# Cross-attention: where the second group of scores stands between the weighted values and the projections of the next batch element

## The chip, the cores and the metric

The kernel runs on one core of a Trainium2 chip. The metric is the device time of one execution in microseconds (us); the median of several runs stands for a kernel. One further execution is taken by the hardware profiler; its trace gives the durations below.

The engines are called PE (matrix products; PEld is its loading of weights), DVE (vector), ACT (scalar, activation functions), POOL (general purpose) and SP (which issues most transfers). Each engine works through its own queue in order, and semaphores join the queues.

## What is computed

A decoder layer in float32: self-attention, cross-attention, and a mixture of experts, each behind a layer norm and each added to the residual. There are 8 batch elements of 112 tokens with 512 features. The change lies in the cross-attention, with 375 context tokens for each element and 32 heads of 16 features:

```python
q = x @ Wq.T
k_raw = context @ Wk.T
v_raw = context @ Wv.T
...
kv = jnp.concatenate([k_raw, v_raw], axis=-1)
kv = kv.reshape(b, m, NHEADS, HEAD_DIM, 2)
k = kv[..., 0].transpose(0, 2, 1, 3)
v = kv[..., 1].transpose(0, 2, 1, 3)
q = _rmsnorm(q)
k = _rmsnorm(k)
scores = jnp.einsum('bhnd,bhmd->bhnm', q, k) * scale
attn = jax.nn.softmax(scores, axis=-1)
out = jnp.einsum('bhnm,bhmd->bhnd', attn, v)
```

## The kernel before

The layer is one program in three stages: self-attention (to about 450 us of the profiled execution), cross-attention (to about 768 us), mixture of experts. In the cross-attention, queries of all tokens, and keys and values of the first element, are made ahead of the loop. The loop at lines 591 to 616 then works on element b and, between its pieces, makes keys and values of element b + 1.

A *pass* of the loop is an element b and a half cp of its 32 heads. A pass has three steps m, one for each third (125 tokens) of the context. Its parts, with the tiles by which the profile names them:

- `exp_scores(b, cp, m)`, line 503: the scores `xs` of 16 heads for one third of the context. A head has only 16 features, so the contraction is short: four strips of 32 rows of the PE array work side by side, each into its own PSUM buffer (line 511). ACT then takes the exponential of each strip (line 519) into a tile `e`. The strips come from the pool `sc`, which has four buffers, so one group of scores takes all of them until the exponentials have read them. The pool of `e` has five buffers (line 390).
- `weigh(b, cp, es)`, line 527: the weighted values `pv` of the pass *before*, from its three tiles `e`. Here the array is split by columns, 32 at a time (line 536). DVE copies the result out (line 551).
- `project_k(b + 1, m)` (line 423) in the first half and `project_v(b + 1, m)` (line 435) in the second: four float32 matmuls of 125 x 512 that use the full array. A key projection is copied out by ACT (`kraw`, line 405), squared by POOL (`sq`, line 407) and summed by DVE (`kss`, line 408); a value projection is copied out by DVE (line 442). The results go through the PSUM pool `mm`, of four buffers.
- `attend(b - 2)`, line 555, from the third element on, in the first half at m = 1: eight transposes `o_t` with the full array (line 561), then division by the softmax sums on DVE and an addition on POOL.
- after a second half, `spread_q(b + 1)` (line 472) and `normed_k(b + 1)` (line 484): the norms of the keys (a square root on ACT, line 411, a reciprocal and three multiplications on DVE) and the transposes `kT` (line 495), which ACT copies out (line 498).

Each matmul instruction of the program is float32 and appears in the profile as two records. A projection is thus "x8" there, a group of scores "x16", the weighted values "x96".

The order of the engines' queues is the program's, but for what a scheduler moves: it places the square root of line 411 and its table load earlier than the program does. On ACT they stand directly behind the third key projection's copy, and so ahead of the exponentials of the next pass, which need a table load of their own (the same instructions stand there for each element; the profile lists seven such loads for line 411).

The order on PE in one pass, when a pass is waiting to be weighted, is:

scores of third 0, weighted values of the pass before, projection 0, scores of third 1 (transposes of `attend`), projection 1, scores of third 2, projection 2.

Of the kernel before, what the change touches and what calls it, by code (L numbers as in the profile page):

```python
# [76 lines left out]
def decoder_layer(  # L77
# [39 lines left out]
    def psum(pool, name):  # L117
        return pool.tile([P, 512], F32, tag=pool.name, name=name)
# [6 lines left out]
    def load_ctx(b):  # L125
        t = ctxpool.tile([P, ND, M], F32, name=f"ctx{b}", tag="ctx")
        with tc.issue_after(first_weights):
            nc.sync.dma_start(out=t, in_=ctxT[b])
        return t
# [10 lines left out]
    def ln_rstd(mv, lo, hi):  # L140
        rs = lnpool.tile([P, TT], F32, tag="rs", name="rs")
        nc.scalar.activation(rs[:, lo:hi], mv[:, lo:hi, 1], AF.Sqrt, bias=eps_ln)
        nc.vector.reciprocal(rs[:, lo:hi], rs[:, lo:hi])
        return rs
# [6 lines left out]
    def ln_apply(mv, rs, t, xnT):  # L151
        xn = ln_normed(mv, rs, t)
        pt = psum(mm, "ln_t")
        for c in range(ND):
            nc.tensor.transpose(pt[:, c * P : (c + 1) * P], xn[:, c * P : (c + 1) * P], ident)
        nc.scalar.copy(xnT[:, :, t * P : (t + 1) * P], pt.rearrange("p (c s) -> p c s", c=ND))
# [227 lines left out]
    with ExitStack() as xa:  # L384
# [11 lines left out]
        ctxs = {0: load_ctx(0)}  # L396
# [6 lines left out]
        def head_squares(ps, n, dst, sums):  # L403

            nc.scalar.copy(dst, ps[:n, :])  # L405
            sq = krp.tile([P, 512], F32, tag="sq", name="sq", bufs=2)
            nc.gpsimd.tensor_tensor(sq[:n], dst, dst, ALU.mult)  # L407
            nc.vector.tensor_reduce(sums, sq[:n].rearrange("p (h d) -> p h d", h=XH), AX.X, ALU.add)
# [5 lines left out]
        def project_k(b, m):  # L414
            if m == 0:
                rawk[b] = (
                    krp.tile([MC, NM, 512], F32, tag="kraw", name="kraw"),
                    krp.tile([MC, NM, XH], F32, tag="kss", name="kss"),
                )
            k, ss = rawk[b]  # L420
            ps = psum(mm, "k")
            for c in range(ND):
                nc.tensor.matmul(  # L423
                    ps[:MC, :],
                    ctxs[b][:, c, m * MC : (m + 1) * MC],
                    wxk[:, c, :],
                    start=(c == 0),
                    stop=(c == ND - 1),
                )
            head_squares(ps, MC, k[:, m, :], ss[:, m, :])  # L430

        def project_v(b, m):
            ps = psum(mm, "xv")
            for c in range(ND):
                nc.tensor.matmul(  # L435
                    ps[:MC, :],
                    ctxs[b][:, c, m * MC : (m + 1) * MC],
                    wxv[:, c, :],
                    start=(c == 0),
                    stop=(c == ND - 1),  # L440
                )
            nc.vector.tensor_copy(
                values[b % 2][:, m, :, :XD], ps[:MC, :].rearrange("p (h d) -> p h d", h=XH)
            )
# [27 lines left out]
        def spread_q(b):  # L472

            queries[b] = qtp.tile([P, ND, 2, S], F32, tag="qT2", name="qT2")
            for e in range(2):
                nc.vector.tensor_scalar(
                    like_seq(queries[b][:, :, e, :], b),
                    seq(xn2, b),
                    cst[:, C_EO + e : C_EO + e + 1],
                    None,  # L480
                    ALU.mult,
                )
# [20 lines left out]
        def exp_scores(b, cp, m):  # L503


            e = ep.tile([MC, 2, 4, 2, S], F32, tag="e", name="e")
            strips = [psum(sc, f"xs{j}") for j in range(4)]
            for ci in range(2):
                for j in range(4):
                    rows = slice(32 * j, 32 * j + 32)  # L510
                    nc.tensor.matmul(  # L511
                        strips[j][:MC, ci * 2 * S : (ci + 1) * 2 * S],
                        keys[b][rows, 2 * cp + ci, m * MC : (m + 1) * MC],
                        queries[b][rows, 2 * cp + ci, :, :],
                        start=True,
                        stop=True,
                    )
            for j in range(4):
                nc.scalar.activation(  # L519
                    e[:, :, j, :, :].rearrange("p c e s -> p c (e s)"),  # L520
                    strips[j][:MC, : 4 * S].rearrange("p (c f) -> p c f", c=2),
                    AF.Exp,
                    scale=float(XD) ** -0.5,
                )
            return e

        def weigh(b, cp, es):


            ps = psum(mm, "pv")  # L530
            v = values[b % 2]
            for g in range(4):
                for m in range(NM):
                    for j in range(4):
                        h = 4 * g + j
                        nc.tensor.matmul(  # L536
                            ps[VW * j : VW * (j + 1), g * S : (g + 1) * S],
                            v[:, m, 16 * cp + h, :],
                            es[m][:, h // 8, (h % 8) // 2, h % 2, :],
                            start=(m == 0),  # L540
                            stop=(m == NM - 1),
                        )
            if cp == 0:
                if b == 0:
                    turned[0] = o0p.tile([P, 2, 4, S], F32, name="oT0")
                else:
                    turned[b] = otp.tile([P, 2, 4, P], F32, tag="oT", name="oT")
                    nc.gpsimd.tensor_copy(
                        turned[b][:, :, :, S:], turned[0][:, :, :, (b - 1) * SP : b * SP]
                    )  # L550
            nc.vector.tensor_copy(
                turned[b][:, cp, :, :S], ps[:, : 4 * S].rearrange("p (g s) -> p g s", g=4)
            )

        def attend(t):

            oT = turned.pop(t + 1)
            for cp in range(2):
                ps = psum(mm, "o_t")
                for g in range(4):  # L560
                    nc.tensor.transpose(ps[:, g * P : (g + 1) * P], oT[:, cp, g, :], ident)
                o = ps.rearrange("p (h d) -> p h d", h=16)
                r = op.tile([P, 16, 1], F32, tag="r", name="r")
                nc.vector.reciprocal(r, o[:, :, XD : XD + 1])
                w = op.tile([P, 16, XD], F32, tag="t", name="t")
                nc.vector.tensor_tensor(w, o[:, :, :XD], r.to_broadcast([P, 16, XD]), ALU.mult)
                half = xs[t][:, cp * 256 : (cp + 1) * 256]
                nc.gpsimd.tensor_tensor(half, half, w.rearrange("p h d -> p (h d)"), ALU.add)
            ln_stats(mv3, t)
# [20 lines left out]
        pending = None  # L590
        for b in range(B):
            for cp in range(2):
                es = []
                for m in range(NM):
                    es.append(exp_scores(b, cp, m))
                    if m == 0 and pending is not None:
                        weigh(*pending)

                    if m == 1 and cp == 0 and b >= 2:
                        attend(b - 2)  # L600
                    if b + 1 < B:
                        if cp == 0:
                            if m == 0:
                                ctxs[b + 1] = load_ctx(b + 1)
                            project_k(b + 1, m)
                        else:
                            project_v(b + 1, m)
                pending = (b, cp, es)
            if b + 1 < B:
                spread_q(b + 1)  # L610
                if b == 5:
                    rs3 = ln_rstd(mv3, 0, 4)
                normed_k(b + 1)
                if b == 5:
                    for t in range(4):
                        ln_apply(mv3, rs3, t, xn3)
# [448 lines left out]
```

## Time and profile before

| What | Value |
|---|---|
| median of 3 runs | 1041.7 us (1040.75 to 1043.2) |
| the profiled execution, its own time | 1046.2 us |
| span of the profiled execution (first to last instruction) | 1044.4 us |
| granted PE clock, mean over the span | 0.991 of full |
| share of the chain that ended last: PE / issue / DVE / DMA | 92% / 3% / 2% / 2% |
| `e` on ACT, line 519 | 192 instructions, 549 ns each, 88.9 us |
| `xs` on PE, line 511 | 768 records, 55.4 us |
| `xv` and `k` on PE, lines 435 and 423 | 192 records each, 88.4 and 87.6 us |
| the loop of the cross-attention | 503.8 to 767.6 us of the span |
| one element in the middle of it (638.05 to 672.60) | 34.55 us, PE busy 34.55, ACT 17.34, DVE 10.82, POOL 4.83 |
| the last element (744.20 to 767.60) | 23.40 us, PE busy 22.39, granted clock 0.78 |

An engine's busy time counts the stretches in which at least one of its instructions runs. PE's matmuls overlap, four at a time where the array is split, so a busy PE is not a PE at its peak. "Granted clock" is the share of the full PE clock that the chip allowed in a stretch. The *chain that ended last* follows the work back from the last instruction, at each step to what released it; the lengths of its pieces on one engine run from start to start, so they can be added. In the order of time, an entry in square brackets at the end of a line is the idle time before the instruction and what ended it.

### The profile page before, as it was taken

The numbers are of one execution on the slowest core, as the hardware profiler recorded it, in microseconds if no ns is written. First come the engines' busy times: TensorE is split into PE (matmuls) and PEld (weight loads), VectorE is DVE, ScalarE is ACT, GpSimd is POOL, SyncE is SP. The second block draws the span as 40 slices with busy tenths as digits, with TensorE's granted clock in tenths as the row PEclk, the third lists the DMA queues.
The fourth block names the chain that finished last, engine by engine and source line by source line (L and its number), as shares of the span: only waits on it lengthen the run. The fifth ranks groups of instructions, "written<-read, shape, count | busy, mean of one in ns | idle before, by whom it ended". The sixth has DMA issues, their size and how long they took to land.

```text
span 1044.4 us, 14683 instructions
## 1 busy us (share of the span) xinstructions
PE 1020.3 (98%) x5760; PEld 540.1 (52%) x5760; DVE 381.8 (37%) x744; ACT 277.4 (27%) x516; POOL 201.3 (19%) x223
## 2 busy tenths in 40 slices
PE   5999999999999999999999999999999989999988
PEld 3556555655565455645555555556665544444433
DVE  3345234522453244654223332242224133333223
ACT  2122011201120013123545554565532011111100
POOL 3241044103410221132100111011053200000041
PEclk9999999999999999999999999999989999999989
DMA  9421002101210120001000000001158247777664
GB/s 347 178 85 46 24 18 83 47 0 41 82 48 1 41 82 8 1 1 41 30 31 31 1 31 30 32 1 41 42 226 323 93 143 226 228 226 230 209 194 121
DMA packets 31092, 95.66 MB, mean 92 GB/s; under 512 B 3888, under 2 KB 5808, under 8 KB 27440
## 3 DMA queue, kind: packets, MB, share of 16 engines
q1 hardware_dynamic: 28272, 86.31, 24.7%
q0 software_dynamic: 2320, 7.63, 2.3%
q8 instruction: 46, 0.75, 0.3%
q10 hardware_dynamic: 432, 0.79, 0.2%
q14 instruction: 22, 0.18, 0.1%
HBM read 78.85 MB, written 14.94 MB: 90 GB/s over the span
## 4 chain that ended last, share of the span: by engine, by line
PE 92%; issue 3%; DVE 2%; DMA 2%; POOL 1%; ACT 0%; SPq 0%; DVEq 0%; POOLq 0%; ACTq 0%
PE qk L256 15%; PE o L343 9%; PE v L333 9%; PE xv L435 8%; PE k L423 8%; PE gu L645 6%; PE xs L511 5%; PE gate L876 4%; PE y L898 4%; PE pv L536 4%; PE up L876 4%; PE ys L924 4%; PE z L221 2%; PE s L186 2%; PE qk L311 1%
## 5 line engine op out<-in xcount | busy, mean ns | idle before, releaser
L519 ACT ACTIVATE e<-xs 125x448 f32<-125x448 f32 x192 | 88.9, 549 | 51.5 <-PE xs L511 51.3
L333 PE MATMUL v<-w,xn 128*128 128x512 f32 x224 | 100.4, 594 | 0.0
L343 PE MATMUL o<-wo,zT 128*128 128x512 f32 x224 | 99.9, 594 | 0.0
L435 PE MATMUL xv<-wx,ctx 128*125 128x512 f32 x192 | 88.4, 603 | 0.0
L423 PE MATMUL k<-wx,ctx 128*125 128x512 f32 x192 | 87.6, 601 | 0.0
L256 PE MATMUL qk<-xc,wc 128*128 128x448 f32 x180 | 70.1, 539 | 0.0
L645 PE MATMUL gu<-xn,sw 128*128 128x448 f32 x176 | 67.5, 540 | 0.0
L343 PEld LDWEIGHTS o<-wo,zT 128*128 128x128 f32 x224 | 41.0, 190 | 44.1 <-issue 44.0
L333 PEld LDWEIGHTS v<-w,xn 128*128 128x128 f32 x224 | 40.7, 190 | 42.1 <-issue 41.1
L407 POOL TENSOR_TENSOR sq<-kraw 125x512 f32<-125x512 f32 x24 | 25.2, 1050 | 184.9 <-ACT kraw L405 184.9
L511 PE MATMUL xs<-qT,kT 32*125 32x224 f32 x768 | 55.4, 380 | 1.0 <-ACT e L519 1.0
L876 PE MATMUL gate<-wex,xT 128*64 x144 | 56.0, 471 | 0.3 <-ACT xT L843 0.3
L423 PEld LDWEIGHTS k<-wx,ctx 128*125 128x125 f32 x192 | 34.3, 187 | 40.1 <-issue 40.1
L207 POOL TENSOR_TENSOR s<-s,sm 112x448 f32<-112x448 f32 x32 | 30.2, 943 | 128.9 <-DVE sm L206 101.3
L435 PEld LDWEIGHTS xv<-wx,ctx 128*125 128x125 f32 x192 | 34.1, 187 | 39.9 <-issue 39.9
L876 PE MATMUL up<-wex,xT 128*64 x144 | 54.4, 459 | 0.0
L511 PEld LDWEIGHTS xs<-qT,kT 32*125 32x125 f32 x768 | 36.6, 184 | 32.1 <-issue 27.6
L831 DVE COPY xn<-wex 128x704 f32 x60 | 31.2, 524 | 57.7 <-PE up L876 57.6
L909 POOL DMA_INDIRECT got<-routed,at x14 | 15.1, 1080 | 190.1 <-DMA routed<-y 186.1
L256 PEld LDWEIGHTS qk<-xc,wc 128*128 128x128 f32 x180 | 34.2, 190 | 33.5 <-issue 32.3
L256 PE MATMUL qk<-xn,w 128*128 128x448 f32 x120 | 50.2, 539 | 0.0
L898 PE MATMUL y<-wd,hT 128*64 128x512 f32 (+1 forms) x216 | 49.5, 592 | 0.6 <-ACT y L902 0.6
(181 smaller groups left out, 1475.2 us busy)
## 6 DMA issues: line engine op xcount, KB each, us to landing
wd<-in_wed_a SPq DMA_DIRECT2D x27, 512.0 KB, 3.7
wex<-in_wegu SPq DMA_DIRECT2D x8, 1408.0 KB, 17.0
wd<-in_wed_b SPq DMA_DIRECT2D x36, 192.0 KB, 4.5
w<-in_wqk SPq DMA_DIRECT2D x6, 1024.0 KB, 4.8
ctx<-in_ctxT SPq DMA_DIRECT2D x8, 750.0 KB, 4.2
slots<-zeros SPq DMA_DIRECT2D x1, 4608.0 KB
xt<-slots SPq DMA_DIRECT2D x18, 256.0 KB, 5.3
wd<-in_wed_a SPq DMA_DIRECT2D x18, 256.0 KB, 4.7
```

Of the source, the lines that this page charges most:

```text
L256: nc.tensor.matmul(ps[:, :HALF], wt[:, c * P : (c + 1) * P], x[:, c, :], start=(c == 0), stop=(c == 1))
L333: nc.tensor.matmul(ps, xn1[:, c, t * P : (t + 1) * P], wv[:, c, :], start=(c == 0), stop=(c == ND - 1))
L343: nc.tensor.matmul(ps, zT[:, h, t * P : (t + 1) * P], wog[:, h, :], start=(h == 0), stop=(h == GH - 1),)
L423: nc.tensor.matmul(ps[:MC, :], ctxs[b][:, c, m * MC : (m + 1) * MC], wxk[:, c, :], start=(c == 0), stop=(c == ND - 1),)
L435: nc.tensor.matmul(ps[:MC, :], ctxs[b][:, c, m * MC : (m + 1) * MC], wxv[:, c, :], start=(c == 0), stop=(c == ND - 1),)
L511: nc.tensor.matmul(strips[j][:MC, ci * 2 * S : (ci + 1) * 2 * S], keys[b][rows, 2 * cp + ci, m * MC : (m + 1) * MC], queries[b][rows, 2 * ...
L519: nc.scalar.activation(e[:, :, j, :, :].rearrange("p c e s -> p c (e s)"), strips[j][:MC, : 4 * S].rearrange("p (c f) -> p c f", c=2), AF.Exp,
L536: nc.tensor.matmul(ps[VW * j : VW * (j + 1), g * S : (g + 1) * S], v[:, m, 16 * cp + h, :], es[m][:, h // 8, (h % 8) // 2, h % 2, :], star ...
L645: nc.tensor.matmul(ps[:, :HALF], w[:, c, i % 2, k, :], xn3[:, c, cols], start=(c == 0), stop=(c == ND - 1))
L876: nc.tensor.matmul(gu[k][n, :FF], xT[:, c, n], w, start=(c == 0), stop=(c == ND - 1))
L898: nc.tensor.matmul(ps[n, :], hT[:fn, i, n], w[i][:fn], start=(i == 0), stop=(i == len(FCH) - 1))
L924: nc.tensor.matmul(p, hidden[n, i, t * P : (t + 1) * P], wsd_t[i // 3][n, i % 3, :], start=(i == 0), stop=(i == 5))
```

## The change

```diff
                     if m == 1 and cp == 0 and b >= 2:
                         attend(b - 2)
                     if b + 1 < B:
-                        if cp == 0:
-                            if m == 0:
-                                ctxs[b + 1] = load_ctx(b + 1)
-                            project_k(b + 1, m)
-                        else:
-                            project_v(b + 1, m)
+                        if cp == 0 and m == 0:
+                            ctxs[b + 1] = load_ctx(b + 1)
+
+
+                        for i in (range(m, m + 1) if pending is None else ((), (0,), (1, 2))[m]):
+                            (project_v if cp else project_k)(b + 1, i)
                 pending = (b, cp, es)
```

Where a pass before is waiting to be weighted (`pending`), step 0 makes no projection, step 1 makes projection 0, and step 2 makes projections 1 and 2. The order on PE in such a pass becomes:

scores of third 0, weighted values of the pass before, scores of third 1 (transposes of `attend`), projection 0, scores of third 2, projections 1 and 2.

The very first pass keeps its order, and the two passes of the last element have no projections. The load of the context stays where it was, at step 0 of the first half. The same instructions are issued. On ACT the copies of the key projections move with them: one behind the exponentials of the second third, two behind those of the last third, and the square root of line 411 with its table load stands behind these two as it stood behind the one. On DVE the sums `kss` and the copies of values move in the same way, and on POOL the squares. SP's queue is the same.

## The prediction

> Names used here: a pass is one (b, cp) of the loop at lines 591 and 592. Its three groups of scores (line 511) are S0, S1, S2, its weighted values (line 536) W, its three projections (line 423 where cp is 0, line 435 where cp is 1) P0, P1, P2. "First" and "second" passes have cp 0 and cp 1.
>
> **What bounds the kernel now.** I read the page's busy times first, then the chain of waits through one batch element, then ScalarE's order of time in the same stretch, then PE's order of time at the last element, and last the granted clock in single stretches.
>
> ```profile
> PE 1020.3 (98%) x5760; PEld 540.1 (52%) x5760; DVE 381.8 (37%) x744; ACT 277.4 (27%) x516; POOL 201.3 (19%) x223
> ```
>
> PE is never free, so whatever PE waits for newly is added to the end, and whatever PE does less of is taken off. The chain of waits (start, length, work; a piece runs to the start of the next) shows what a group costs and in which order they stand:
>
> ```profile
> 645.15 0.97 PE xs L511 x16
> 646.12 1.02 PE o_t L561 x8
> 647.14 3.43 PE k L423 x8
> 650.58 0.97 PE xs L511 x16
> 651.54 3.63 PE k L423 x8
> 655.17 0.97 PE xs L511 x16
> 656.14 2.44 PE pv L536 x96
> 658.57 3.63 PE xv L435 x8
> ```
>
> The reader should see two things. The same eight matmuls of a projection take 3.63 us behind scores and 3.43 us behind the transposes o_t, which use the same full array: changing the array's shape costs 0.20 us. And in the second pass, which begins at 655.17, S0 and W are over 3.40 us later; P0 comes next, and S1 only at 662.20.
>
> ScalarE in the same stretch (start, length, line, what):
>
> ```profile
> 639.16 1.85 ACT L519 ACTIVATE e<-xs 125x448 f32<-125x448 f32 x4 [0.33 <-PE xs L511]
> ...
> 655.21 0.59 ACT L405 COPY kraw<-k 125x512 f32<-125x512 f32 x1 [1.74 <-PE k L423]
> 655.81 1.28 ACT L411 ACT_TABLE_LOAD   x1
> 657.73 0.38 ACT L411 ACTIVATE kss<-kss,eps_rms 125x96 f32<-125x96 f32 x1 [0.64 <-DVE kss L408]
> 658.12 1.28 ACT L519 ACT_TABLE_LOAD   x1
> 659.42 1.85 ACT L519 ACTIVATE e<-xs 125x448 f32<-125x448 f32 x4
> ```
>
> This is what decides. In the first pass (S0 at 638.12) the four exponentials run at once and end at 641.01, just before W ends at 641.52. In the second pass they stand behind the copy of the last key projection, the square root of its norms and two table loads: they end at 659.42 + 1.85 = 661.27, that is 2.70 us after W's piece has ended (2.77 against PE's own start of the next group, 658.50, as the chain dates its pieces 0.07 later). The scores' PSUM pool has four buffers and each group fills all four, so S1 can't start until the exponentials of S0 free them, strip by strip. Today P0, 3.63 us long, covers that.
>
> PE's order of time at the last element, which has no projections, shows both outcomes:
>
> ```profile
> 747.59 1.04 PE L511 MATMUL xs<-qT,kT 32*125 32x224 f32 x16
> ...
> 761.33 2.93 PE L511 MATMUL xs<-qT,kT 32*125 32x224 f32 x16 [0.67 <-ACT e L519]
> 764.18 3.52 PE L536 MATMUL pv<-e,v 125*32 125x112 f32 x96
> ```
>
> At 747.59 S1 stands directly behind W, unhindered, at the usual length. At 761.33 scores stand directly behind scores: PE waits 0.67 us and then starts each strip 0.05 us after the exponential that frees it (the first ended at 761.27).
>
> **The change, part by part.** Sixteen passes; the very first keeps its order, the two of the last element have no projections, so 13 change: 6 first ones (b = 1 to 6) and 7 second ones (b = 0 to 6). Instructions are the same in kind and number.
>
> *Removed: one change of shape.* S0, W, P0, S1, P1, S2, P2 become S0, W, S1, P0, S2, P1+P2; the transposes of line 561 stay behind S1, next to a projection. The new step from W to S1 costs no more than the others (the group at 747.59 has its usual 1.04). 13 x 0.20 = 2.6 us less.
>
> *New: S1 directly behind W.* In the six first passes the fourth exponential is over 0.44 us before W is (641.01 against 641.45, PE's own start of the next group; at b = 6, where ScalarE has LayerNorm copies ahead, 0.76): no wait. In the seven second passes the fourth exponential ends 2.70 us (b = 0, 1) or 2.77 us (b = 2 to 6) after PE could start S1. That end is unmoved by the change: it hangs on the end of P2 of the pass before, through copy, square, sum, square root and loads, and in the changed kernel's order ScalarE still has copy, copy, load, square root, load, exponentials there. With 0.05 us for the release, less the 0.02 us by which the fourth strip starts after the first anyway, the wait is 2.73 or 2.80 us: 2 x 2.73 + 5 x 2.80 = 19.5 us. Behind the waiting matmuls stand P0, S2, P1 and P2 on the in-order PE; nothing gives this back, since PE has no idle time later in the element.
>
> *New: the clock.* Waiting may cost more than its length. The stretches below (length, busy times, granted clock, DMA):
>
> ```profile
> 759.49:762.91 3.42, 2.75 (x34) 1.83 (x30) 0.62 (x1) 1.85 (x4) 0.00 (x0) 1.00 0.00 0
> 762.91:766.32 3.41, 3.41 (x58) 2.81 (x58) 0.00 (x0) 2.68 (x5) 0.00 (x0) 0.50 0.00 0
> 844.83:848.24 3.41, 1.94 (x12) 0.70 (x8) 1.49 (x3) 0.46 (x1) 0.00 (x0) 1.00 0.83 252
> 848.24:851.65 3.41, 2.53 (x17) 1.46 (x18) 0.53 (x1) 0.59 (x1) 0.00 (x0) 1.00 0.27 58
> ```
>
> The clock changes on a grid of 3.41 us. In the first stretch PE was idle for 0.67 us and then ran one strip of four for 1.31 us (each busy 0.37 of 0.43 us, so 0.21 of the array: 1.03 us of array time lost): 1.70 us lost, and the next stretch got half the clock. In the third 3.41 - 1.94 = 1.47 us were lost and the clock stayed. The threshold lies between. The predicted wait loses 1.51 us idle (658.50 to 660.01, the first release), 1.03 in the trickle and 0.28 in the tail of the fourth strip: 2.8 us. Only a grid line that splits it so that neither side passes the threshold spares it. With the threshold at 1.70 that is a line 1.12 to 1.75 us into the wait, 0.63 of 3.41 us, so 82% trip; at 1.47 it is 0.12 us, 96%. I take the middle, 89% or 6.2 of 7. A trip's price from the same place: W took 3.52 for the usual 2.51 us (+1.0), and the scores before it reached W 1.55 us after their last release (762.63) where 0.95 is usual (+0.6): 1.6 us; bounds are 1.5 and the 1.71 of a whole stretch at half. 6.2 x 1.6 = 10.0 us, between 8.6 (5.7 x 1.5) and 11.5 (6.7 x 1.71).
>
> [...] The trace shows half clock after stretches that were idle for only 0.67 us, so I go by the row.
>
> *Moved at no cost.* P1 and P2 stand together, with the four-buffer pool of line 117 under them: the buffer that each takes belonged to work that ended over 2 us earlier, against copies of 0.6 to 0.7 us. The copies of keys on ScalarE come after S2's exponentials (1.85 us), inside P1's 3.43. The element's last projection still ends where the next S0 starts, so the norms, the transposes kT and the next keys are due as before. POOL's squares stand three in a row behind its additions, about 1.04 us each against 3.43 us a projection; SP's order, with the context load, is unchanged. A fifth buffer for exponentials exists for S1 (five are named at line 390). If one of these covers failed it would cost at most the 0.6 us of a copy in a pass.
>
> **Sum.** -2.6 + 19.5 + 10.0 = +26.9 us. The profiled execution took 1046.2 us (span 1044.4) and would become 1073.1; it lies 4.5 us over the median of the runs, 1041.7, which becomes 1068.6.
>
> **Rivals.**
> - *The wait alone, full clock* (16%): 1041.7 - 2.6 + 19.5 = 1058.6. For it: the 1.47 us stretch that didn't trip. Against it: two trips at the last element with 0.33 and 0.67 us of plain idleness.
> - *Each trip lasts two stretches* (11%): the first trip at the last element held from 752.67 to 759.49, 6.82 us. 6.2 x 3.3 = 20.5, so 1079. Against it: there scores still trickled in its first stretch, here a dense projection follows.
> - *No wait, only the saved shape* (3%): 1041.7 - 2.6 = 1039.1. It decides if S0's exponentials in the second passes end by 658.5 and not 661.3, so if the square root and its loads, 2.9 us of ScalarE's time with the sum they wait for, leave that place. For it: S1 at 747.59 and the six first passes. Against it: the order named above.
> - *No measurable change* (2%): the waits are eaten by slack that I don't see; PE's idle time in the whole span is 24 us, 1044.4 - 1020.3, and hardly any lies here.
>
> **How the numbers follow.** The forecast has 68%, with its own range 1065 to 1072 (the trips' bounds, and 1.5 us for the runs' spread of 1040.75 to 1043.2). The range must take in the second-likeliest case at 1058.6 and stops short of the two-stretch case: 1057 to 1074. A difference under 0.2% (2 us) can't be told from none. Faster 3%, within 2%, slower 95%.
>
> **What would show it.** In the chain: W followed by xs with an idle entry released by ACT e at every second pass, 1.5 us, groups of about 3.8 us with their wait in place of 0.97, none in first passes; P1+P2 as one piece of 16 matmuls and 7.06 us; granted clock 0.50 for 3.41 us after most of the seven. Busy PE times grow where the clock halves. I am wrong if the second passes show no such idle entry, or if the clock stays at 1.00 through them.

## The result, and the profile after

The changed kernel took 1072.99 us (median of 6 runs, 1069.59 to 1074.99), the kernel before 1041.22 (6 runs, 1039.59 to 1044.59): 1.0298 of it, 95% interval 1.0271 to 1.0324, so 31.8 us more. Foretold were +26.9 us, 1068.6, within 1057 to 1074; the measured time lies above the 1065 to 1072 that the forecast gave to its likeliest case. The profiled execution of the changed kernel has a span of 1071.0 us, that of the kernel before 1044.4. These two differ by only 26.6 us, because the profiled execution of before (1046.2 us) was slower than every one of its six timed runs; the closeness to 26.9 is chance. In two runs below a single execution took 2128 and 3033 us at full clock; the medians given leave these two out.

The names are those of the prediction: S0, S1, S2 are a pass's groups of scores, W its weighted values, P0 to P2 its projections. PE's order of time in the changed kernel shows one second pass (cp = 1, from 671.87) and the start of the next element; columns are start, length, engine, line, operation, and in brackets the idle time before it and who ended it:

```profile
671.87 1.04 PE L511 MATMUL xs<-qT,kT 32*125 32x224 f32 x16
672.84 2.51 PE L536 MATMUL pv<-e,v 125*32 125x112 f32 x96
676.72 2.55 PE L511 MATMUL xs<-qT,kT 32*125 32x224 f32 x16 [1.37 <-ACT e L519]
679.20 5.12 PE L435 MATMUL xv<-wx,ctx 128*125 128x512 f32 x8
684.25 1.04 PE L511 MATMUL xs<-qT,kT 32*125 32x224 f32 x16
685.22 7.13 PE L435 MATMUL xv<-wx,ctx 128*125 128x512 f32 x16
692.18 1.45 PE L495 MATMUL kT<-cst,kraw 125*128 125x125 f32 x12
693.56 1.04 PE L511 MATMUL xs<-qT,kT 32*125 32x224 f32 x16
694.53 2.51 PE L536 MATMUL pv<-e,v 125*32 125x112 f32 x96
696.97 1.04 PE L511 MATMUL xs<-qT,kT 32*125 32x224 f32 x16
```

S1 at 676.72 has the idle entry that was foretold (1.37 us, where 1.5 was expected), and takes 2.55 us for the usual 1.04: its four strips start one by one, 0.43 to 0.44 us apart (676.72, 677.15, 677.59, 678.03). P0 behind it takes 5.12 us for the usual 3.70. P1 and P2 are one piece of 16 records. The next first pass (693.56) has W and S1 back to back and no wait.

The chain of waits ran on PE alone through this loop before, up to the last element. Now it leaves PE once in each second pass as well, and names every step that the exponentials waited for:

```profile
666.79 5.16 PE k L423 x12
671.95 0.02 issue
671.98 0.59 ACT kraw L405
672.57 0.07 issue
672.64 1.05 POOL sq L407
673.69 0.02 issue
673.71 0.70 DVE kss L408
674.41 0.03 issue
674.43 0.02 ACT kss L411
674.46 0.37 issue
674.83 1.28 ACT L519
676.11 0.01 issue
676.12 0.55 ACT e L519
676.67 0.04 issue
676.72 2.55 PE xs L511 x16
679.27 5.05 PE xv L435 x8
```

From the end of P2, 671.95, it runs over the keys' copy, square, sum, square root (dated as issue, 674.46) and table load to the first exponential, then to S1. S0 and W, which PE works off meanwhile (672 to 675.3), are not in the chain: they have become the shorter way.

The profile records when the granted clock changed. In the changed kernel it went between 1.00 and 0.50 at 18 times, from 521.67 to 1033.67 us of the span, and any two of these lie a whole number of times 3.41 us apart; so do the 7 times in the kernel before, from 752.67 to 1042.80. These times, carried on every 3.41 us through a profile, are called its grid here; the word describes these records and no more.

The windows (length, then busy times of PE, PEld, DVE, ACT, POOL with their numbers of instructions, granted clock, DMA share, GB/s), first the second passes of b = 0, 1 and 2, then four stretches of the grid about the wait of b = 1:

```profile
515.23:536.91 21.68, 20.31 (x181) 11.61 (x180) 6.76 (x11) 9.83 (x18) 1.04 (x1) 0.92 0.02 3
552.94:576.32 23.38, 22.01 (x181) 12.20 (x180) 6.76 (x11) 9.82 (x18) 1.04 (x1) 0.85 0.03 4
593.18:614.87 21.69, 20.32 (x182) 11.48 (x181) 6.77 (x11) 9.83 (x18) 1.04 (x1) 0.92 0.02 3
...
555.81:559.22 3.41, 2.04 (x38) 1.35 (x30) 3.18 (x5) 3.20 (x6) 0.00 (x0) 1.00 0.00 0
559.22:562.63 3.41, 3.41 (x13) 1.79 (x13) 0.00 (x0) 1.85 (x4) 0.00 (x0) 0.50 0.01 2
562.63:566.05 3.42, 3.42 (x5) 1.32 (x4) 0.00 (x0) 0.00 (x0) 0.00 (x0) 0.50 0.00 0
566.05:569.46 3.41, 3.41 (x23) 1.63 (x22) 1.51 (x3) 1.34 (x4) 0.00 (x0) 1.00 0.00 0
```

A second pass took 17.51 us before (551.43 to 568.94 at b = 1). It takes 21.7 us where the clock was halved for one stretch and 23.4 where it was for two, as here from 559.22 to 566.05. Over the loop, from its first scores to the end of the last W, the profiles give 263.7 us before (503.92 to 767.63) and 294.45 after (501.44 to 795.89), +30.7 us. It comes together like this, all from PE's starts:

| Where | Change, us |
|---|---|
| six first passes, 0.19 to 0.20 each (at b = 1, 16.22 became 16.03) | -1.2 |
| seven second passes: +4.17, 5.87, 4.18, 5.77, 4.19, 5.69, 4.24 | +34.1 |
| the last element, 744.18 to 767.63 became 774.67 to 795.89 | -2.2 |

Of the +34.1, the waits are 7 x 2.75 = 19.3 (at b = 6, where the clock fell only after the wait, P0 starts 2.72 us late; at b = 2, 2.77), the saved changes of shape -1.4, and what is left, 16.2, is put down to the clock (the runs with useless work, below, check this): four passes with one slow stretch (1.6 us each), three with two (3.1 to 3.3).

### The profile page after: what moved, and what is told of

The parts are those of the page before. It is cut to its first block, busy times and chain, and to the rows that moved or that the text cites. A ratio compares the mean times of both kernels' runs of the same rounds, so it can differ in the third digit from the quotient of the medians.

```text
span 1071.0 us, 14683 instructions
## 1 busy us (share of the span) xinstructions
PE 1037.4 (97%) x5760; PEld 550.0 (51%) x5760; DVE 382.1 (36%) x744; ACT 277.4 (26%) x516; POOL 200.9 (19%) x223
## 4 chain that ended last, share of the span: by engine, by line
PE 86%; issue 5%; ACT 2%; DMA 2%; DVE 2%; POOL 2%; SPq 0%; DVEq 0%; POOLq 0%; ACTq 0%
PE qk L256 15%; PE o L343 9%; PE v L333 9%; PE xv L435 8%; PE k L423 6%; PE gu L645 6%; PE xs L511 5%; PE gate L876 4%; PE y L898 4%; PE up L876 4%; PE ys L924 3%; PE pv L536 2%; PE z L221 2%; PE s L186 2%; POOL sq L407 2%
## 5 line engine op out<-in xcount | busy, mean ns | idle before, releaser
L435 PE MATMUL xv<-wx,ctx 128*125 128x512 f32 x192 | 99.7, 674 | 0.0
L511 PE MATMUL xs<-qT,kT 32*125 32x224 f32 x768 | 66.4, 389 | 10.6 <-ACT e L519 10.6
L435 PEld LDWEIGHTS xv<-wx,ctx 128*125 128x125 f32 x192 | 39.7, 215 | 51.5 <-issue 51.5
L511 PEld LDWEIGHTS xs<-qT,kT 32*125 32x125 f32 x768 | 43.3, 186 | 37.8 <-issue 18.6
L442 DVE COPY v<-xv 125x512 f32<-125x512 f32 x24 | 16.6, 692 | 93.8 <-PE xv L435 93.8
## 6 DMA issues: line engine op xcount, KB each, us to landing
slots<-zeros SPq DMA_DIRECT2D x1, 4608.0 KB, 19.3
```

The lines of the kernel that those rows point to most:

```text
L435: nc.tensor.matmul(ps[:MC, :], ctxs[b][:, c, m * MC : (m + 1) * MC], wxv[:, c, :], start=(c == 0), stop=(c == ND - 1),)
L511: nc.tensor.matmul(strips[j][:MC, ci * 2 * S : (ci + 1) * 2 * S], keys[b][rows, 2 * cp + ci, m * MC : (m + 1) * MC], queries[b][rows, 2 * ...
```

## Experiments

Two theories were set against each other. *Wait and clock*: in second passes S1 waits for exponentials that stand on ScalarE behind the square root of the keys' norms, and the granted clock goes to 0.50 after the wait, as it did after the two waits of the last element before. *Neighbours*: what now stands side by side (scores behind weighted values, two projections in a row with their copies) costs something of its own in every changed pass. Each ratio is to runs of the kernel before on the same chip.

**First passes alone.**

```diff
-for i in (range(m, m + 1) if pending is None else ((), (0,), (1, 2))[m]):
+for i in (range(m, m + 1) if pending is None or cp == 1 else ((), (0,), (1, 2))[m]):
```

> The new order in the first passes alone (cp = 0, six of them); the second passes keep the order of before. If the loss is the wait for the exponentials behind the square root (with the halved clock after it), the first passes never wait and only six changes of shape at 0.20 us are saved: 1041.2 - 1.2 = 1040.0 us, no idle entry before a group of scores up to the last element, clock 1.00 there. If instead the new neighbours cost something of their own (scores directly behind the weighted values, or two projections in a row with their copies), six of thirteen passes pay it: 1041.2 + 6/13 x 31.8 = 1056 us.

Measured: 1040.33 us (12 runs), 0.9984 of the kernel before (0.9968 to 0.9999). In the element from 637 to 672 us PE has no idle entry, and the granted clock was 0.998 over the span, as one stretch of 3.41 us at 0.50 makes it. Six passes in the new order are a small gain, by about the six changes of shape (0.0016 x 1042 = 1.7 us, interval 0.1 to 3.3, for 1.2 expected). In first passes the neighbours cost nothing.

**Second passes alone.** The same edit with `cp == 0`.

> The new order in the second passes alone (cp = 1, seven of them). If the loss is the wait and the clock: seven waits of 2.8 us and seven trips as in the changed kernel, less seven changes of shape only: 1073.0 + 1.2 = 1074 us, give or take 3 us for where the clock's grid falls. If the neighbours cost: 1041.2 + 7/13 x 31.8 = 1058 us.

Measured: 1073.67 us (median of 3 runs), 1.0295 (1.0263 to 1.0326): the whole loss, in seven passes of thirteen. One of the seven waits went by at full clock; the windows are the two stretches of that profile's grid about it:

```profile
677.33:680.74 3.41, 1.97 (x65) 1.58 (x55) 2.93 (x5) 2.77 (x5) 0.00 (x0) 1.00 0.00 0
680.74:684.15 3.41, 3.41 (x19) 2.00 (x19) 0.82 (x2) 2.58 (x6) 0.00 (x0) 1.00 0.00 0
```

The grid line, 680.74, fell 2.03 us into the wait (W was over at 678.71): 1.51 idle and 0.52 x 0.79 = 0.41 of trickle, 1.92 us of array time lost ahead of it by the prediction's count, and the clock stayed at 1.00.

**The square root later.** The changed kernel, with ScalarE's square root of the keys' norms ordered behind the exponentials of the second pass's S0:

```diff
...
+    with tc.issue_after(last_exp[b - 1, 1, 0]):
+        nc.scalar.activation(flat_kss, flat_kss, AF.Sqrt, bias=eps_rms[:MC], scale=1.0 / XD)
...
```

> The changed kernel with one more order on ScalarE: the square root of the keys' norms, with its table load, stands behind the exponentials of the second pass's first group of scores and no longer ahead of them. All instructions stay. If that place is the cause, the exponentials end 2.97 us after the group's start, before the weighted values are over at 3.40 us: no wait, no halved clock in the seven passes, all thirteen changes of shape saved: 1041.2 - 2.6 = 1038.6 us. If the neighbours or the projections in a row cost, it stays at 1073 us. If only half of the wait goes (the loads then hold up the second group's exponentials against the third scores, margin by my sum 0.2 us), between 1040 and 1050 us.

Measured: 1038.44 us (12 runs), 0.9968 (0.9954 to 0.9983). No instruction was added or taken, nothing on PE was reordered against the changed kernel, and over 30 us are gone. The chain of waits in a second pass is PE's alone again:

```profile
653.20 0.97 PE xs L519 x16
654.17 2.44 PE pv L544 x96
656.60 0.97 PE xs L519 x16
657.57 3.63 PE xv L435 x8
661.20 0.97 PE xs L519 x16
662.16 7.06 PE xv L435 x16
```

S1 (656.60) follows W at once, in 0.97 us. ScalarE in that stretch has the exponentials at 654.24, and the loads and the square root behind them:

```profile
654.24 1.85 ACT L527 ACTIVATE e<-xs 125x448 f32<-125x448 f32 x4 [0.42 <-PE xs L519]
656.11 1.28 ACT L491 ACT_TABLE_LOAD   x1
657.41 0.38 ACT L491 ACTIVATE kss<-kss,eps_rms 125x96 f32<-125x96 f32 x1
657.80 1.28 ACT L527 ACT_TABLE_LOAD   x1
659.10 1.85 ACT L527 ACTIVATE e<-xs 125x448 f32<-125x448 f32 x4
```

**The control: the same on the kernel before.**

> The control: the kernel before with the square root moved in the same way. There the first projection of 3.63 us already covers the exponentials, so nothing waits for the square root: 1041.2 us, no change within 1 us. If moving the square root were a gain of its own, it would show here as in the run beside it: about 1038.6 us.

Measured: 1042.05 us (median of 11 runs), 0.9999 (0.9981 to 1.0017). The place of the square root is worth nothing by itself. What the last two runs together show is the change without its wait: a gain of about 3 us, for 2.6 worked out.

**Useless work in the wait.** The changed kernel, with matmuls between W and S1 of the second passes whose result nobody reads:

```diff
+if cp == 1 and b + 1 < B:
+    idle = psum(mm, "idle")
+    for _ in range(3):
+        nc.tensor.matmul(idle, ctxs[b][:, 0, :P], wxv[:, 0, :], start=True, stop=True)
```

> The changed kernel with useless work in the wait: in the seven second passes three more matmuls of 128 x 512 with the full array (six records of 0.43 us, and a change of shape of 0.20, so 2.77 us) between the weighted values and the second group of scores; their result is not read. If the wait of 2.8 us and the clock are the loss, this work takes the wait's place and keeps PE busy: no idle entry, no halved clock in the seven passes: 1041.2 - 2.6 + 7 x 2.8 = 1058 us, so more work and 15 us less time than the changed kernel. If the loss were work of PE's own (shape changes, neighbours), the 19 us of added work come on top: 1092 us.

> The same with two useless matmuls (1.72 us and one change of shape, 1.92). The wait that is left is 0.88 us and falls into the trickle of the strips; the second group still starts its fourth strip at the same time, so the sum is again 1058 us, and by the threshold of 1.47 to 1.70 us of lost array time no clock is halved (0.88 x 0.79 + 0.28 = 1.0 us lost). If a trip needs no such threshold, 10 us more.

> The same with one useless matmul (0.86 us and one change of shape, 1.06). The wait that is left loses 0.45 us idle, 1.03 in the trickle and 0.28 in the tail, 1.76 us: just over the threshold, and only if one grid stretch holds nearly all of it. Few trips, 0 to 3 of seven: 1058 to 1063 us. If the length of the plain idle time decided, and not the array time lost, 0.45 us would never trip; if any wait tripped, seven would: 1069 to 1074 us.

Measured, in this order: 1059.37 us, 1.0165 (1.0136 to 1.0194); 1056.89 us, 1.0151 (1.0117 to 1.0186); 1060.74 us, 1.0175 (1.0147 to 1.0203). All three take some 12 to 16 us less than the changed kernel, though each does more. PE's order with three and with one such matmul, and the clock with three and with one, from 500 to 762 us, which takes in all seven of these passes' waits:

```profile
665.77 2.51 PE L536 MATMUL pv<-e,v 125*32 125x112 f32 x96
668.20 2.84 PE L601 MATMUL idle<-wx,ctx 128*128 128x512 f32 x6
670.98 1.04 PE L511 MATMUL xs<-qT,kT 32*125 32x224 f32 x16
671.94 3.70 PE L435 MATMUL xv<-wx,ctx 128*125 128x512 f32 x8
```

```profile
665.71 2.51 PE L536 MATMUL pv<-e,v 125*32 125x112 f32 x96
668.15 1.12 PE L601 MATMUL idle<-wx,ctx 128*128 128x512 f32 x2
669.59 2.32 PE L511 MATMUL xs<-qT,kT 32*125 32x224 f32 x16 [0.32 <-ACT e L519]
671.85 3.70 PE L435 MATMUL xv<-wx,ctx 128*125 128x512 f32 x8
```

```profile
500.00:762.00 262.00, 262.00 (x2467) 144.40 (x2465) 75.68 (x136) 128.17 (x240) 30.89 (x38) 1.00 0.07 24
```

```profile
500.00:762.00 262.00, 259.76 (x2439) 144.92 (x2437) 75.65 (x136) 128.19 (x240) 30.89 (x38) 1.00 0.07 24
```

P0 starts as late as ever (three: 671.94 - 665.77 = 6.17 us after W's start; one: 6.14; the changed kernel's P0 679.20 - 672.84 = 6.36, part of it at half clock), but takes 3.70 us, and the clock is 1.00 through all seven waits. This separates the two terms: with the wait's length kept and the clock kept up, the loss is about 17 us; the rest of the 31.8, some 15, is the clock's. By passes it comes out the same: with one useless matmul a second pass, from its W to the next (six of the seven; the other holds LayerNorm work), takes 2.73 us more than in the run with the later square root (20.04 against 17.31), the wait alone; in the changed kernel it takes 21.7 or 23.3. With one useless matmul, idleness and trickle still lose 1.7 us a pass (estimated with the prediction's count), and the clock was halved after none of the seven waits.

**Useful work in the wait.** P0 of the second passes in halves, two of its four matmuls ahead of S1:

```diff
...
+if cp == 1 and b + 1 < B:
+    project_v(b + 1, 0, range(2))
...
+if cp and i == 0:
+    project_v(b + 1, 0, range(2, ND))
...
```

> The changed kernel with useful work in the wait: in the seven second passes the first two of projection 0's four matmuls stand between the weighted values and the second group of scores, the other two behind it. Seven groups of one shape again in these passes. 1.72 + 0.20 us of the wait are covered, 0.88 is left, no halved clock: 1041.2 - 1.2 + 7 x 0.88 = 1046 us. If the two projections in a row at the pass's end were a loss of their own, it would stay above 1055 us.

Measured: 1043.94 us (10 runs), 1.001 (0.999 to 1.003). S1 takes 1.85 us for 1.04 in the second passes (0.81 x 7 = 5.7 us, less 1.2 for the shapes), and in its profile the clock was full over the whole loop, the last element too (1.0 over the span), where the profile of before loses time to two trips. That explains in these two executions why it cost less than foretold (the loops take 264.5 and 263.7 us); the other runs were not profiled. P1 and P2 in a row do no harm here either.

**The lesson tried on the last element.** It has no projections, so its own S0 waits for the exponentials of S2. The last third of its value projection was kept back to stand between them, on top of the later square root:

```diff
...
+if cp and b + 1 == B - 1 and i == 2:
+    continue
...
+elif cp == 0 and m == 2:
+    project_v(b, m)
```

> The changed kernel with the square root later (as in the run before), and the same lesson used on the last element, which has no projections to cover its exponentials: the last third of its own value projection (due only in the second pass of that element) stands behind the third group of scores of its first pass, and no longer in the element before. If a wait for exponentials costs its length and a halved clock, the wait between these two groups of scores (0.33 us idle and the trickle, 1.6 us in all) and the first of the two trips there (about 1.6 us) go, and two changes of shape come in (0.4 us): 2.8 us under the run beside it, 1035.6 us. If the last element's slow clock is not the waits' doing, only 1.2 us.

> The kernel with the square root later once more, on the same chip as the run beside it: 0.9968 of the kernel before, about 1038.5 us.

Measured: 1037.13 us, 0.9941 (0.992 to 0.9962), beside 1036.10 us, 0.9936 (0.9913 to 0.9959), for the kernel without it: no gain in the time. In the profiles it is there at first: the last W of the loop ends at 759.72 instead of 762.39, 2.7 us earlier where 2.8 were foretold, with no halved clock in that element (granted clock 1.00 from 740 to 770 us, beside 0.94). But the experts' stage then runs two slow stretches more of 3.41 us than the kernel beside it (from 841.5 us on one, from 995.0 two for one; granted clock 0.97 beside 0.99 from 840 to 1000 us, 0.93 beside 0.98 from there on), and the spans are 1037.7 and 1037.4. Whether that is chance in these two executions or follows from the shifted start is open; the runs' medians show no gain.

The fastest kernel found is thus the change with the square root later: 0.9968 and 0.9936 of the kernel before on two chips, 1038.44 and 1036.10 us. The last kernel (0.9941) can't be told from it.

## Why the prediction was right, and what it mis-sized

*The change of shape, -2.6 us.* Right: 0.19 to 0.20 us less in each first pass, and the run with the later square root gains about that over its control.

*The wait, +19.5 us.* Right: 7 x 2.75 = 19.3. It was read from where the fourth exponential stood against the end of W in the trace of before, and from the order on ScalarE, which the change leaves alone. The first passes, where 0.44 us of margin were read, never waited.

*Only in second passes, and for the square root's sake.* Right, and shown: the loss stays with the second passes alone, leaves with the square root's place, and that place is worth nothing without the change.

*The clock, +10.0 us, between 8.6 and 11.5.* That the waits would be followed by half the clock was right (seven waits with 1.37 us of plain idle time each, granted clock 0.50 in the next stretch after all seven), and the size was not: 16.2 us. Two steps failed.

- "A trip's price from the same place ... 1.6 us; bounds are 1.5 and the 1.71 of a whole stretch at half" held for four of seven. Three trips lasted two stretches and cost 3.1 to 3.3 us. The prediction had this as a rival that holds for all trips or for none. What goes with the one or the other is where the grid's line fell in the wait. In the changed kernel, lines 2.41 to 2.87 us into the wait (three) went with two slow stretches, and lines 3.04 to 4.27 us into it (four) with one. In the three, P0 starts only 1.56 to 2.12 us into the first slow stretch, with the rest of S1 before it; in the four, at most 1.24 us into it.
- "82% trip; at 1.47 it is 0.12 us, 96%" took the grid's line as drawn anew for each wait, and 1.47 to 1.70 us of lost array time as what decides. The upper bound was mis-sized: 1.70 counted only the idleness and the trickle of its stretch, and in the run with second passes alone 1.92 us by the same count left the clock at 1.00. An estimate from the two traces of before and after counts every matmul record for as long as its columns take (0.43 us for 512 at full clock, as in a projection) and for its share of the array; it gives 2.19 us for the prediction's stretch. By this estimate, of 160 stretches of the grid at full clock from 500 to 800 us in the two profiles, the ten that were followed by a halved one had lost 2.19 to 2.71 us of their 3.41, and the other 150 at most 1.82. With 1.92 to 2.19 us in place of 1.47 to 1.70 the prediction's own sum gives 54 to 70% for a wait (an estimate: 2.8 us lost in all, spared by a line in 1.04 to 1.58 of 3.41 us), so four or five of seven. But the waits aren't independent. In the changed kernel a single slow stretch makes an element 38.55 us long, 11.29 times 3.41; a double one 40.2, 11.78 times. So the line moves 1.0 us earlier in the wait after a single and 0.75 later after a double: up to the LayerNorm work it swings between 2.41 and 3.60 us. In the profile single and double alternate, and all seven waits are followed by half the clock.

*The last element* was taken as unchanged. It got 2.2 us shorter, with one slow stretch of 3.41 us (from 784.50) where it had three (two from 752.67, one from 762.91). That offset part of the clock's excess: -2.6 + 19.3 + 16.2 - 2.2 = 30.7, as in the profiles.

*Luck.* The measured 1073.0 lies 1.0 us inside the range, because the three waits with two slow stretches brought it only part of the way to the rival of two stretches each, 1079. That the phase mixed the two was not foreseen.

*The rivals.* "The wait alone, full clock", 1058.6, is what the useless work produced: 1056.9 to 1060.7 us, with the granted clock at 1.00 through the waits in the two profiles shown. "No wait, only the saved shape", 1039.1, is what the later square root produced, 1038.4: the point named there, exponentials over before W is, is the point that decides. (Its 2.9 us are the two loads and the square root alone; with the 0.64 us in which the square root waited for the sum they are 3.6.)

## What to carry to other kernels

Before work is moved off a place, ask what it covered there, on every kind of pass: here two passes of one loop had the same order on PE, but only one of them had a square root and two table loads ahead of the exponentials. Read the order on the engine that frees the buffers, not its share of the time: ScalarE was busy for 27% of the span and still set the end. And price a wait on PE with the clock that it costs behind it: here seven waits cost 19.3 us by their length and, by difference, 16.2 by the halved clock. Where such waits recur, the price of one may not be a mean over all phases: here one and two slow stretches alternated, by the length of the element that each left.

## What was not expected of the hardware

- PE's busy time alone did not say whether the clock would be halved. After the stretch from 555.81, with PE busy for 2.04 of 3.41 us, much of it with one strip of four at work, the granted clock was 0.50; in the kernel before, after the one from 844.83, with 1.94 of 3.41 us busy and its products in pairs of 64 columns of the array each, started within 0.01 us of each other, it stayed at 1.00.
- Adding 18 us of useless matmuls (7 x 2.57) made the changed kernel some 14 us faster (1072.99 to 1059.37), with the granted clock at 1.00 from 500 to 762 us.
- The slow stretches of the loop fell into step with its elements: in the changed kernel they begin 37.55 and 40.96 us apart, which is 11 and 12 times 3.41, in turn (only the last distance, over the element with the LayerNorm work, is 44.37, 13 times).
